# Three-pass gate products in every step, head rows scaled by another engine, and a new order of the whole run: a four-layer graph network on one core

## The chip, the cores and the metric

One Trainium2 chip, one core of it. The metric is the device time of one launch in microseconds (us). PE is the matrix engine, DVE the vector engine, ACT the scalar engine, POOL the general one, SP the engine whose queue issues nearly all transfers here. PSUM is the memory that PE writes, in eight banks[...].

## The reference, cut to what matters

Input `x` is 32 batches of 512 nodes with 128 features, and one 512x512 adjacency matrix serves all of them. Four layers follow each other, each as `x = x + layer(relu(layernorm(x)))`.

```python
# layer 0, once a batch
out = einsum('nm,bmc->bnc', A_norm, h);  out = out @ W.T + b
# layer 1, five steps a batch (in_matrix and out_matrix are both adj)
m = einsum('nm,bmd->bnd', adj, h);  av = concat([m, m]);  u3 = h @ u3_w.T + u3_b
z = sigmoid(av @ w3_w.T + w3_b + u3);  r = sigmoid(av @ w4_w.T + w4_b + u3)
hv = tanh(av @ w5_w.T + w5_b + (r * h) @ u5_w.T + u5_b)
h = (1 - z) * h + z * hv
# layers 2 and 3, attention over the edges
h = h @ W;  e = leaky_relu(e_src[:, None] + e_dst[None, :]);  softmax over the neighbours;  attn @ h
```

## The kernel before, in words

Each batch is a tile of 128x512 numbers. Layer 0 (`gcn`) and layer 1 (`ggnn`, `step`) are products with the adjacency, and layers 2 and 3 (`gat`) are attention. In all four, PE does the products, ACT what comes out of PSUM and the tanh and exp, DVE the sums and products of whole tiles and the transposes of 32x32 blocks (L592), which DMAs through DRAM finish (`shuttle`).

A product with 32-bit operands is taken at full precision (an FP32 matmul) or in three passes of reduced precision (FP32R). For three passes the moving operand is split (`operands`, L615 to L618): ACT writes `upper`, a little below the operand; DVE writes `lower`, the rest, and `across`, a mix of both. The fixed operand has been split once in the same way. PE adds the products of the uppers and of the lowers in a bank, ACT rescales the bank in place (`rescale`, L624), and PE adds the product of the across tiles. The product with the adjacency is always taken so (`in_three`, L642).

In `step`, that product, called `m`, goes into the three gate products of r, z and the candidate (`by_m`), each with a 128x128 weight. Where (batch, step) is in `SPLIT_GATES` (L29), `in_three` gives back the three split tiles instead of `m`, and the gate products are taken in three passes; elsewhere ACT copies `m` out of the bank (L653), and each gate product is a full-precision one. The products of `hT` and `rh` with their weights are at full precision in all steps (all of these run on L753). r and z share a bank: after r has been read, a split step rescales the bank back (factor 1/(1 + 1/4096)), and the product for z is added to it. Then DVE makes `rh` (L785), ACT the tanh of r, z and the candidate (L783, L790, L794), and DVE the new state (L796, L797, L799). Before the change, 84 of the 160 steps are split: steps 0, 2 and 4 of batches 2 to 29.

In `gat`, PE multiplies by the head weights (L866) into two banks of two chunks each. ACT takes the exp of three score columns (L882). In all but the last four batches, DVE then multiplies each pair of 128x128 chunks by its first exp column (L884). In the last four batches ACT does that scaling, one chunk at a time (L879). DVE makes the edge weights `e` (L907), and PE the mix (L933 and, in the last batches, L919).

The order of all instructions is fixed before the kernel runs, by the class `Plan`. Every operation has an engine, a cost and a due time, written beside it in the code. `attempt` plays the run with those costs. At each moment an engine takes the ready operation with the smallest `soon`, if buffers for it are free: eight banks, four tiles each of `upper` and `lower`, five of `across`, nine of `x`, six lanes. In the first round `soon` is the due time (or less, for operations with a long tail). In later rounds `put_off` plays the run backwards, and `soon` comes from how late each operation may be; only operations that lie after `near_end` in the plan's time (1228) take that value, and the others keep the due time. There are six rounds for each of two settings, and the order that ends first in the plan is emitted. Each engine then works through its queue in exactly that order, and waits where an operand or a buffer is not there yet. The plan's costs are 0.858 for a full-precision product of 512 columns (`MM`), 0.2325 for one pass (`MR`), 0.595 for a DVE operation on a whole tile (`V`), and 0.495 for an ACT copy (`COPY`).

The functions that the change touches, and what calls them:

Of the kernel before, what the change touches and what calls it, by code (L numbers as in the profile page):

```python
# [10 lines left out]
F32 = mybir.dt.float32  # L11
# [14 lines left out]
IDLE_FROM = 1342  # L26
RUN_UP = 8
LANES = 6
SPLIT_GATES = {(b, s) for b in range(2, 30) for s in range(STEPS) if s % 2 == 0}  # L29

# [27 lines left out]
class Plan:  # L60
# [44 lines left out]
    def run(self):  # L105


        self.before = {o: [] for o in self.ops}
        for o in reversed(self.ops):
            o.tail = o.cost + o.delay + max((q.tail for q in o.then), default=0)  # L110
            o.first, o.after = o.waits, len(o.then)
            for q in o.then:
                self.before[q].append(o)
        self.uses = {v: v.uses for o in self.ops for v in o.vals}
        best = math.inf, None
        for last, hurry in self.ends:
            for again in range(6):
                if again:
                    late = self.put_off()
                for o in self.ops:  # L120
                    if not again:

                        o.soon = min(o.due, last - o.tail * hurry)
                    else:
                        o.soon = late[o] / self.SLOT if o.at > self.near_end else o.due
                self.attempt()
                if self.end < best[0]:
                    best = self.end, [o.soon for o in self.ops]
                if self.end == math.inf:
                    break  # L130
        assert best[1], "the order has come to a stop"
        for o, soon in zip(self.ops, best[1]):
            o.soon = soon
        self.attempt()
        for o in self.order:
            o.emit()
# [134 lines left out]
def gnn_stack(ctx: ExitStack, tc: tile.TileContext, a: dict, out: bass.AP):  # L271
# [13 lines left out]
    def flat(t):  # L285
# [31 lines left out]
        "rstd": tiles(8, SMALL, "rstd"),  # L317
        "off": tiles(6, SMALL, "off"),
        "rden": tiles(3, SMALL, "rden"),
    }, [(167, 0.1), (181, 0.05)], 1228,  # L320
        IDLE_FROM, lambda v: nc.tensor.transpose(v.t[:, 0, :], ident.t, ident.t))
    op = plan.op
    MM, MM1, TURN, MR = 0.858, 0.224, 0.111, 0.2325
# [288 lines left out]
    def operands(src, given, made, due):  # L612

        upper, lower, across = Val("upper"), Val("lower"), Val("across")
        op("ACT", COPY, due - 5, lambda: nc.scalar.mul(made(upper.t), given(src.t), BELOW), r=[src], w=[upper])  # L615
        op("DVE", V, due - 5, lambda: nc.vector.tensor_sub(made(lower.t), given(src.t), made(upper.t).bitcast(F32)),  # L616
           r=[src, upper], w=[lower])
        op("DVE", V, due - 5, lambda: nc.vector.scalar_tensor_tensor(  # L618
            flat(across.t), flat(lower.t).bitcast(F32), -SPLIT, flat(upper.t).bitcast(F32), op0=ALU.mult, op1=ALU.add),
           r=[lower, upper], w=[across])  # L620
        return upper, lower, across
# [126 lines left out]
    def step(b, s, m, hT, due, lane):  # L748
        gate, r, rh, z, cand = Val("bank"), Val("r"), Val("rh"), Val("z"), Val("bank")
        split = isinstance(m, tuple)  # L750

        def weigh(p, i, moving, start=False, of=None):
            nc.tensor.matmul(flat(p.t), (of or gates).t[:, i, :], flat(moving.t), start=start, stop=True, skip_group_check=True)  # L753

        def by_m(p, i, at, start, *more):

            rest = [x for _, _, reads in more for x in reads]

            def others():
                for of, moving, _ in more:  # L760
                    weigh(p, 0, moving, of=of)
            if not split:
                def whole():
                    weigh(p, i, m, start)
                    others()
                op("PE", (1 + len(more)) * MM, at, whole, r=[m, gates, *rest], w=[p])
                return
            upper, lower, across = m
            upper_of, lower_of, across_of = of_gates

            def first_two():
                weigh(p, i - 1, upper, start, upper_of)
                weigh(p, i - 1, lower, False, lower_of)

            def third_one():
                weigh(p, i - 1, across, False, across_of)
                others()
            op("PE", 2 * MR, at, first_two, r=[upper, lower, upper_of, lower_of], w=[p])
            rescale(p, at - 5)
            op("PE", MR + len(more) * MM, at, third_one, r=[across, across_of, *rest], w=[p])  # L780

        by_m(gate, 1, due + 0.2, True, (gates, hT, [hT, gates]))
        op("ACT", A, due - 5, lambda: nc.scalar.activation(flat(r.t), flat(gate.t), AF.Tanh, bias=gate_b["w4"].t, scale=0.5),  # L783
           r=[gate, gate_b["w4"]], w=[r])
        op("DVE", V, due - 5, lambda: nc.vector.scalar_tensor_tensor(flat(rh.t), flat(r.t), 1.0, flat(hT.t), op0=ALU.add, op1=ALU.mult),  # L785
           r=[r, hT], w=[rh])
        if split:
            rescale(gate, due - 5, 1 / (1 + 1 / SPLIT))
        by_m(gate, 2, due + 0.3, False)
        op("ACT", A, due - 5, lambda: nc.scalar.activation(flat(z.t), flat(gate.t), AF.Tanh, bias=gate_b["w3"].t, scale=0.5),  # L790
           r=[gate, gate_b["w3"]], w=[z])
        hv, new = Val("hv"), Val("hT")
        by_m(cand, 3, due + 0.4, True, (u5T, rh, [rh, u5T]))
        op("ACT", A, due - 5, lambda: nc.scalar.activation(flat(hv.t), flat(cand.t), AF.Tanh, bias=gate_b["w5"].t),  # L794
           r=[cand, z, gate_b["w5"]], w=[hv])
        op("DVE", V, due - 5, lambda: nc.vector.tensor_sub(flat(hv.t), flat(hv.t), flat(hT.t)), r=[hT], w=[hv])  # L796
        op("DVE", V, due - 5, lambda: nc.vector.scalar_tensor_tensor(flat(hv.t), flat(z.t), 1.0, flat(hv.t), op0=ALU.add, op1=ALU.mult),  # L797
           r=[z], w=[hv])
        op("DVE", V, due - 5, lambda: nc.vector.scalar_tensor_tensor(flat(new.t), flat(hv.t), 0.5, flat(hT.t), op0=ALU.mult, op1=ALU.add),  # L799
           r=[hv, hT], w=[new])  # L800

        last = s == STEPS - 1
        h = Val("h", C)
        if not EARLY <= due < STEPS * B:
            p = to_features(new, due + 2, *([] if last else [h]))
            if last:
                op("DVE", V, due + 2, lambda: nc.vector.tensor_add(flat(xs[b].t), flat(xs[b].t), flat(p.t)),
                   r=[p, lane], w=[xs[b]])
            else:
                op("ACT", COPY, due + 1, lambda: nc.scalar.copy(flat(h.t), flat(p.t)), r=[p], w=[h])  # L810
            return h, False, new
        shuttle(new, "p (c q i) -> p q c i", h, due, due - 5)
        if last:
            op("DVE", V, due + 2, lambda: nc.vector.tensor_add(
                xs[b].t.rearrange("p c (k j) -> p k c j", k=Q), xs[b].t.rearrange("p c (k j) -> p k c j", k=Q),
                h.t.rearrange("p k (c j) -> p k c j", c=C)), r=[h, lane], w=[xs[b]])
        return h, True, new
# [27 lines left out]
    def gat(b, l, due):  # L845
# [14 lines left out]
        for a, q in enumerate(qs):  # L860
# [7 lines left out]
            if near:  # L868
                def scores(a=a, qt=qt, ht=ht):
                    for c in range(2):  # L870
                        nc.scalar.activation(ht()[:, c, D:D + 3], qt()[:, c, D:D + 3], AF.Exp,
                                             scale=rstd.t[:, 2 * a + c:2 * a + c + 1])
                op("ACT", 0.2, due + 1, scores, r=[q, rstd], w=[h[2 + a]])
                op("DVE", 0.08, due + 1, lambda a=a, ht=ht: nc.vector.tensor_mul(
                    g.t[:, 2 * a:2 * a + 2], ht()[:, :, D], rstd.t[:, 2 * a:2 * a + 2]), r=[rstd, h[2 + a]], w=[g[a]])

                def scale(a=a, qt=qt, ht=ht):
                    for c in range(2):
                        nc.scalar.mul(ht()[:, c, :D], qt()[:, c, :D], g.t[:, 2 * a + c:2 * a + c + 1])  # L879
                op("ACT", 2 * 0.385, due + 1.5, scale, r=[q, g[a]], w=[h[a]])  # L880
            else:
                op("ACT", 0.1, due + 1, lambda qt=qt, ht=ht: nc.scalar.activation(ht()[:, :, D:D + 3], qt()[:, :, D:D + 3], AF.Exp),  # L882
                   r=[q], w=[h[2 + a]])
                op("DVE", 0.335, due + 1.5, lambda qt=qt, ht=ht: nc.vector.tensor_mul(  # L884
                    ht()[:, :, :D], qt()[:, :, :D], ht()[:, :, D:D + 1].to_broadcast([P, 2, D])), r=[q, h[2 + a]], w=[h[a]])
        exps = [h[2], h[3]]

        row, e, mask = Val("row"), Val("e", C), (own_mask if near else maskT)[l]
# [134 lines left out]
```

## Time and profile before

| | us |
|---|---|
| median of 3 runs (1555.43 to 1557.11) | 1556.69 |
| the profiled execution, its own time | 1555.74 |
| its span, first to last instruction | 1554.0 |
| PE idle in the first 100 us | 4.96 |
| PE idle in the last 54 us | 5.4 |
| PE idle in the 1400 us between | 7.2 |

The span is the part of the time in which instructions run. An engine's busy time is the time in which at least one of its instructions is under way; instructions of one engine overlap at their ends, and a matmul's end is modelled, so a busy engine can still be held up inside it. A row of the groups gives line, engine, operation, output<-inputs, shapes, count, then busy time and mean duration of one, and the idle time of the engine just before with what ended it. A row of the timeline gives start, length, engine, line, operation, tiles and how many were merged. A row by stage gives the stretch and then, for each engine, busy us and instructions. A full-precision matmul is two records in the trace, a reduced-precision pass one. The granted PE clock is full in every slice.

### The profile page before, as it was taken

Reading aid. Unit: us, or ns where it says so; the run is one execution under the profiler, and the core shown is the slowest. Engines: PE = TensorE matmul, PEld = TensorE weight load, DVE = VectorE, ACT = ScalarE, POOL = GpSimd, SP = SyncE. Lnnn points to the kernel's source line nnn. Section 1 sums busy time; section 2 is a strip of 40 time slices with the busy share of each in tenths; the row PEclk is TensorE's granted clock in tenths of the full one; section 3 lists DMA queues with packets and bytes.
Section 4 is the critical chain, followed back from the end, with each engine's and each line's share of the span. In section 5 each row is a group of like instructions: output and inputs, shape, how many; then the busy total and the mean of one; then the engine's idle time right before and its main releaser. Section 6 shows DMA issues by size and latency. Waiting matters only on the chain.

```text
span 1554.0 us, 23910 instructions
## 1 busy us (share of the span) xinstructions
PE 1536.5 (99%) x7213; PEld 1118.2 (72%) x7213; DVE 1450.7 (93%) x3725; ACT 1048.0 (67%) x2160; POOL 155.1 (10%) x137
## 2 busy tenths in 40 slices
PE   9999999999999999999999999999999999999998
PEld 7665677777767777776777767777767776767778
DVE  8999889899999999999999999999999989978789
ACT  7867776666677576766757667676776658466574
POOL 2201000010011010111100110101010101000010
PEclk9999999999999999999999999999999999999999
DMA  3143344444354444434344444344343434523101
GB/s 109 42 99 105 78 101 114 108 117 110 95 136 108 119 114 108 124 102 122 96 111 115 122 111 114 99 120 116 102 130 90 115 92 110 131 72 105 44 13 42
DMA packets 270147, 157.72 MB, mean 101 GB/s; under 512 B 81249, under 2 KB 236225, under 8 KB 270017
## 3 DMA queue, kind: packets, MB, share of 16 engines
q1 hardware_dynamic: 269728, 155.66, 38.7%
q8 instruction: 57, 0.93, 0.3%
q10 hardware_dynamic: 288, 0.52, 0.1%
q14 instruction: 74, 0.60, 0.1%
HBM read 86.25 MB, written 69.84 MB: 100 GB/s over the span
## 4 chain that ended last, share of the span: by engine, by line
PE 62%; DVE 26%; ACT 4%; DMA 3%; issue 3%; SPq 1%; POOL 1%; DVEq 0%; POOLq 0%; ACTq 0%
PE bank L753 27%; PE bank L642 21%; PE bank L933 9%; DVE e L907 3%; DVE lower L616 3%; DVE st L507 2%; DVE across L618 2%; PE bank L866 2%; DVE sq L592 2%; DVE hv L797 1%; DVE hv L796 1%; DVE hT L799 1%; ACT bank L624 1%; POOL rstd L520 1%; DVE rh L785 1%
## 5 line engine op out<-in xcount | busy, mean ns | idle before, releaser
L624 ACT ACTIVATE bank<-bank 128x512 f32<-128x512 f32 x524 | 295.6, 582 | 174.3 <-PE bank L642 126.0
L520 POOL TENSOR_TENSOR rstd<-ve,mhalf 128x4 f32<-128x4 f32 x119 | 142.9, 1202 | 1310.9 <-DVE ve L512 954.1
L753 PE MATMUL bank<-m,wT 128*128 128x512 f32 x456 | 225.4, 595 | 4.6 <-ACT r L783 2.5
L933 PEld LDWEIGHTS bank<-h_gat,e 128*128 128x128 f32 x1792 | 210.2, 191 | 16.1 <-issue 11.0
L933 PE MATMUL bank<-h_gat,e 128*128 128x129 f32 x1792 | 212.0, 275 | 0.7 <-DVE v L938 0.4
L642 PE MATMUL bank<-adj,across 128*128 128x512 f32 x640 | 192.1, 426 | 1.1 <-ACT bank L624 1.1
L642 PE MATMUL bank<-adj,upper 128*128 128x512 f32 x640 | 192.7, 423 | 0.0
L618 DVE SCALAR_TENSOR_TENSOR across<-lower,upper 128x512 fp32r<-128x512 f32 x272 | 183.1, 678 | 3.9 <-PE bank L753 1.9
L642 PE MATMUL bank<-adj,lower 128*128 128x512 f32 x640 | 173.2, 393 | 0.0
L753 PE MATMUL bank<-rh,wT 128*128 128x512 f32 x320 | 164.0, 594 | 0.2
L753 PE MATMUL bank<-hT,wT 128*128 128x512 f32 x320 | 163.3, 592 | 0.0
L783 ACT ACTIVATE r<-bank,gate_bw 128x512 f32<-128x512 f32 x160 | 109.6, 685 | 75.4 <-PE bank L753 72.3
L907 DVE SCALAR_TENSOR_TENSOR e<-row,h_gat,maskT 128x512 f32<-128x512 f32 x224 | 157.6, 741 | 0.0
L642 PEld LDWEIGHTS bank<-adj,across 128*128 128x128 f32 x640 | 118.4, 188 | 50.3 <-issue 19.4
L642 PEld LDWEIGHTS bank<-adj,upper 128*128 128x128 f32 x640 | 118.5, 188 | 42.3 <-issue 18.9
L790 ACT ACTIVATE z<-bank,gate_bw 128x512 f32<-128x512 f32 x160 | 109.0, 685 | 51.1 <-PE bank L753 49.4
L642 PEld LDWEIGHTS bank<-adj,lower 128*128 128x128 f32 x640 | 120.0, 188 | 27.6 <-DVE lower L616 0.7
L794 ACT ACTIVATE hv<-bank,gate_bw 128x512 f32<-128x512 f32 x160 | 108.9, 685 | 41.8 <-PE bank L753 41.4
L526 ACT ACTIVATE y<-x,off,rstd 128x128 f32<-128x128 f32 x252 | 111.4, 488 | 31.9 <-DVE off L523 30.5
L796 DVE TENSOR_TENSOR hv<-hv,hT 128x512 f32<-128x512 f32 x160 | 108.6, 682 | 21.3 <-ACT hv L794 21.2
L753 PEld LDWEIGHTS bank<-m,wT 128*128 128x128 f32 x456 | 82.0, 189 | 63.8 <-issue 37.3
L753 PE MATMUL bank<-upper,gates 128*128 128x512 f32 x252 | 124.7, 495 | 0.9 <-ACT bank L624 0.9
(159 smaller groups left out, 2622.8 us busy)
## 6 DMA issues: line engine op xcount, KB each, us to landing
far<-sq SPq DMA_DIRECT2D x928, 64.0 KB
h<-far SPq DMA_DIRECT2D x148, 256.0 KB
gT<-far SPq DMA_DIRECT2D x56, 256.0 KB
row<-line SPq DMA_DIRECT2D x56, 256.0 KB
hT<-far SPq DMA_DIRECT2D x112, 64.0 KB
x<-in_x_dram SPq DMA_DIRECT2D x24, 256.0 KB
out_dram<-x SPq DMA_DIRECT2D x20, 256.0 KB
adjT<-in_x_dram SPq DMA_DIRECT2D x8, 256.0 KB
```

What stands on the lines that cost most here:

```text
L520: op("POOL", 1.0, due, lambda: nc.gpsimd.tensor_tensor(rstd.t, ve.t, mhalf.t, ALU.pow), r=[ve, mhalf], w=[rstd])
L526: op("ACT", 0.385, due, lambda c=c: nc.scalar.activation(chunk(y, c), xb.t[:, c, :], AF.Relu, bias=off.t[:, c:c + 1], scale=rstd.t[:, c:c ...
L618: op("DVE", V, due - 5, lambda: nc.vector.scalar_tensor_tensor(flat(across.t), flat(lower.t).bitcast(F32), -SPLIT, flat(upper.t).bitcast(F ...
L624: op("ACT", COPY, due, lambda: nc.scalar.mul(flat(p.t), flat(p.t), by), w=[p])
L642: nc.tensor.matmul(flat(p.t), left.t[:, c, :], right.t[:, c, :], start=first and c == 0, stop=c == C - 1, skip_group_check=True)
L753: nc.tensor.matmul(flat(p.t), (of or gates).t[:, i, :], flat(moving.t), start=start, stop=True, skip_group_check=True)
L783: op("ACT", A, due - 5, lambda: nc.scalar.activation(flat(r.t), flat(gate.t), AF.Tanh, bias=gate_b["w4"].t, scale=0.5), r=[gate, gate_b["w ...
L790: op("ACT", A, due - 5, lambda: nc.scalar.activation(flat(z.t), flat(gate.t), AF.Tanh, bias=gate_b["w3"].t, scale=0.5), r=[gate, gate_b["w ...
L794: op("ACT", A, due - 5, lambda: nc.scalar.activation(flat(hv.t), flat(cand.t), AF.Tanh, bias=gate_b["w5"].t), r=[cand, z, gate_b["w5"]], w ...
L796: op("DVE", V, due - 5, lambda: nc.vector.tensor_sub(flat(hv.t), flat(hv.t), flat(hT.t)), r=[hT], w=[hv])
L907: op("DVE", 0.65, due + 3, lambda j=j: nc.vector.scalar_tensor_tensor(e.t[:, j, :], matrix(row), h.t[:, j, D + 1:D + 2], mask.t[:, j, :], ...
L933: nc.tensor.matmul(pt()[:, c, :D + 1], e.t[:, j, i * P:(i + 1) * P], h.t[:, j, :D + 1], start=(j == 0), stop=(j == C - 1))
```

## The change

Four edits. `SPLIT_GATES` takes all five steps of batches 2 to 29, so 140 steps instead of 84 are split. The scaling of head rows in all but the last four batches goes from one DVE operation for two chunks to two ACT operations, one for each chunk. `near_end` goes from 1228 to 0, so that the backward pass gives every operation's priority, and there are eight rounds instead of six. The plan's cost of `lower` and `across` goes from 0.595 to 0.575. The function `one_pass` stands for `weigh` in the split products and issues the same matmuls.

```diff
-SPLIT_GATES = {(b, s) for b in range(2, 30) for s in range(STEPS) if s % 2 == 0}
+SPLIT_GATES = {(b, s) for b in range(2, 30) for s in range(STEPS)}
...
-            for again in range(6):
+            for again in range(8):
...
-    }, [(167, 0.1), (181, 0.05)], 1228,
+    }, [(167, 0.1), (181, 0.05)], 0,
...
-        op("DVE", V, due - 5, lambda: nc.vector.tensor_sub(made(lower.t), given(src.t), made(upper.t).bitcast(F32)),
+        op("DVE", 0.575, due - 5, lambda: nc.vector.tensor_sub(made(lower.t), given(src.t), made(upper.t).bitcast(F32)),
...
-        op("DVE", V, due - 5, lambda: nc.vector.scalar_tensor_tensor(
+        op("DVE", 0.575, due - 5, lambda: nc.vector.scalar_tensor_tensor(
             flat(across.t), flat(lower.t).bitcast(F32), -SPLIT, flat(upper.t).bitcast(F32), op0=ALU.mult, op1=ALU.add),
...
+        def one_pass(p, i, moving, start, of):
+            nc.tensor.matmul(flat(p.t), of.t[:, i - 1, :], flat(moving.t), start=start, stop=True, skip_group_check=True)
...
-                weigh(p, i - 1, upper, start, upper_of)
-                weigh(p, i - 1, lower, False, lower_of)
+                one_pass(p, i, upper, start, upper_of)
+                one_pass(p, i, lower, False, lower_of)
...
-                weigh(p, i - 1, across, False, across_of)
+                one_pass(p, i, across, False, across_of)
...
-                op("DVE", 0.335, due + 1.5, lambda qt=qt, ht=ht: nc.vector.tensor_mul(
-                    ht()[:, :, :D], qt()[:, :, :D], ht()[:, :, D:D + 1].to_broadcast([P, 2, D])), r=[q, h[2 + a]], w=[h[a]])
+                def scale(qt=qt, ht=ht):
+                    for c in range(2):
+                        nc.scalar.mul(ht()[:, c, :D], qt()[:, c, :D], ht()[:, c, D:D + 1])
+                op("ACT", 0.52, due + 1.5, scale, r=[q, h[2 + a]], w=[h[a]])
```

## The prediction, made before the changed kernel was run

> **What bounds the kernel now.** I read the page's busy times first, then the busy times by stage, the groups by line, and the timeline for the distance between starts.
>
> ```profile
> span 1554.0 us, 23910 instructions
> PE 1536.5 (99%) x7213; PEld 1118.2 (72%) x7213; DVE 1450.7 (93%) x3725; ACT 1048.0 (67%) x2160; POOL 155.1 (10%) x137
> PE 62%; DVE 26%; ACT 4%; DMA 3%; issue 3%; SPq 1%; POOL 1%; DVEq 0%; POOLq 0%; ACTq 0%
> ```
>
> PE is busy 99%, DVE 93%. The chain that ended last runs mostly through PE, and already a quarter of it through DVE. By stage, cut where the 26th and the 126th `rh` (L785) start in the timeline (252.1 and 1187.7 us, 100 gated steps or 20 batches apart), and for three single windows:
>
> ```profile
> core 0: us, PE busy (x) PEld busy (x) DVE busy (x) ACT busy (x) POOL busy (x), PEclk, DMA share, GB/s
> 0.00:252.00 252.00, 246.37 (x998) 168.30 (x998) 225.44 (x618) 184.03 (x363) 34.38 (x35) 1.00 0.36 90
> 252.00:1188.00 936.00, 931.41 (x4358) 682.22 (x4357) 899.97 (x2271) 641.87 (x1308) 90.73 (x77) 1.00 0.44 113
> 1188.00:1554.00 366.00, 358.68 (x1861) 267.66 (x1859) 325.28 (x838) 222.12 (x491) 30.03 (x25) 1.00 0.30 81
> ...
> 400.00:500.00 100.00, 99.96 (x459) 72.11 (x458) 98.03 (x251) 70.84 (x146) 11.03 (x9) 1.00 0.43 111
> 1000.00:1100.00 100.00, 100.00 (x465) 72.69 (x464) 98.04 (x257) 71.24 (x146) 10.87 (x9) 1.00 0.43 110
> ```
>
> In the middle 60% of the run DVE is busy 900 of 936 us, against 89% before and after it. DVE there has 36 us to spare, and the change takes from it. The groups concerned:
>
> ```profile
> L624 ACT ACTIVATE bank<-bank 128x512 f32<-128x512 f32 x524 | 295.6, 582 | 174.3 <-PE bank L642 126.0
> L753 PE MATMUL bank<-m,wT 128*128 128x512 f32 x456 | 225.4, 595 | 4.6 <-ACT r L783 2.5
> L618 DVE SCALAR_TENSOR_TENSOR across<-lower,upper 128x512 fp32r<-128x512 f32 x272 | 183.1, 678 | 3.9 <-PE bank L753 1.9
> L884 DVE TENSOR_TENSOR h_gat<-bank,h_gat 128x256 f32<-128x256 f32 x112 | 44.0, 409 | 0.8 <-ACT h_gat L882 0.7
> ```
>
> Rows overlap, so a mean is too long as a price; the distance between starts is the price:
>
> ```profile
> 700.07 1.88 PE L753 MATMUL bank<-m,wT 128*128 128x512 f32 x4
> ...
> 703.12 0.40 PE L753 MATMUL bank<-upper,gates 128*128 128x512 f32 x1
> ...
> 703.23 0.68 DVE L618 SCALAR_TENSOR_TENSOR across<-lower,upper 128x512 fp32r<-128x512 f32 x1
> 703.35 0.40 PE L753 MATMUL bank<-lower,gates 128*128 128x512 f32 x1
> ...
> 703.83 0.74 DVE L907 SCALAR_TENSOR_TENSOR e<-row,h_gat,maskT 128x512 f32<-128x512 f32 x1
> ```
>
> Four `m,wT` records take 1.88 us, so (1.88 - 0.595)/3 = 0.428 each; one full-precision product is two records, 0.857. A reduced-precision pass is 703.35 - 703.12 = 0.23. `across` holds DVE for 703.83 - 703.23 = 0.60, not 0.678.
>
> [...]
>
> **The change, part by part.**
>
> *Gate products on PE.* 28 batches x 2 odd steps x 3 gates = 168 products[...]: 168 x (0.857 - 3 x 0.23) = 168 x 0.167 = 28 us off PE. All on the bound engine.
>
> *What feeds them.* For each of the 56 steps: the copy of `m` (L653, 584 ns) becomes `upper<-bank` (L615, 593 ns), a wash; `lower` and `across` on DVE are new, 56 x 2 x 0.60 = +67 us; four rescales of a bank (L624; three in by_m, one that undoes it between r and z) are new on ACT, 224 x 0.49 (a pair of them lasts 1.07, one 0.58) = +110 us. Each rescale lies between two PE groups on one bank; queued behind it on ACT are tanh and relu of other lanes, for which DVE's `rh` and `hv` wait.
>
> *Head rows.* 112 DVE operations go: two `h_gat` rows together last 0.72 in the timeline, one 0.41, so about 0.32 each: -36 us on DVE. Instead ACT gets 224 scalings of 128x128 from a bank. The last four batches do that already (L879, mean 371 ns, two in a row 0.63): 0.26 each, +58 us. ACT: 1048 + 110 + 58 = 1216 us, near 79%; it stays below the other two, and costs only where its order delays someone.
>
> *DVE in sum*: +67 - 36 = +31 us, of which 20/28 or 22 in the middle stretch.
>
> *The order.* The change from 1228 to 0 lets the backward pass set the priorities of every operation, not only of late ones, and two tries are added. Instruction counts of DVE (3727), SP (1464) and POOL (142) are the same in the two built programs, so no transfer is added; all are moved. On SP the load of the w4 weights goes from third to seventh, behind two x loads and the W load; its transposes stand ahead of PE's first product (8.71 us now), so up to 1 us may be lost, or nothing if it lands in time. For the order as such I see no gain: counting passes, PE is filled 97.6% from 400 to 1200 us and about 97% from 1250 to 1500, where the backward pass worked already. Value 0, ends -6 (half of the 12 us that PE lacks work before 252 us) and +6. The costs that the planner has for `lower` and `across` fall to 0.575; the trace says 0.60, so the plan believes DVE some 600 x 0.025 = 15 us freer than it is. The pools of `upper` and `lower` stay at four for 328 uses instead of 272: 18.8 us for a use instead of 22.9. Price unknown: 0 to +8.
>
> **The sum, by stage.** I counted the instructions on each engine's queue in the two orders up to the same `rh`, and priced them with the starts above (e 0.66, transposes 0.63, bn_stats 0.19, 128-column products 0.22).
> - To the 26th `rh`: PE 239.6 before, 238.7 after. 252.1 becomes about 251.5.
> - Middle: PE 919 falls to 898, DVE 883 rises to 902 (busy 900 is longer than 883 because some 0.08 us of a row's end shows only when nothing follows it). Now PE fills 98.2% of the 935.6 us and DVE 94.3%. Afterwards DVE has more work than PE. It becomes the bound. I let it reach 97.5%, a little less than the bound engine does today, since PE must be kept at 898/925 = 97.1% at the same time; the windows from 400 and 1000 show both near that. 902/0.975 = 925 us, 11 less.
> - Rest: PE 347.5 falls to 340.1, DVE 312 rises to 321 and keeps slack: 366.3 x 340.1/347.5 = 358.5, 8 less.
>
> 251.5 + 925 + 358.5 = 1535 of span. The profiled execution took 1555.74 for a span of 1554.0, so 1.7 is outside; and it lay 0.95 below the median of 1556.69. 1535 + 1.7 + 1.0 = about 1538.
>
> **The rivals.**
> - *PE stays the bound*, DVE follows: the middle is 898/0.982 = 914, total 251.5 + 914 + 358.5 + 2.7 = 1527. For it: single 50 us stretches with DVE at 99%. Against it: 902 us of DVE in 914 is 98.7%.
> - *Looser*: DVE reaches only 96%: 902/0.96 = 940, total 1552, a third of a per cent.
> - *Slower: ACT's order starves DVE.* Each newly split step puts four more rescales on ACT's one queue, and `upper`, which opens DVE's two new operations, stands on that queue too. If DVE's filling stays at today's 94.3%, the middle is 902/0.943 = 956 and the total 1569. It decides when the filling is below 902/944 = 95.6%, at which the 8 us won at the end are eaten. For it: ACT goes from 67% to 79%, the plan underrates DVE. Against it: today DVE idles because PE is the bound, not because ACT is late (r L783 kept `rh` waiting only 13.7 us in all).
> - *The change does not do what it says*: ruled out; the built program has 420 products in three passes instead of 252, and 60 full-precision ones from `m` instead of 228.
>
> **How the numbers follow.** DVE-bound 1538: 0.43; PE-bound 1527: 0.22; looser 1552: 0.17; slower 1569: 0.18. A measurement tells 0.2% (3 us) from no change. Faster: 0.43 + 0.22 + 0.12 of the looser case = 0.77; same 0.05; slower 0.18. The range goes from the PE-bound case less the -6 of the order, 1522, to 1559, above the looser case with most of the pools' +8; it leaves out most of the slower case.
>
> **What would show it.** Right: 28 us less PE passes, DVE busy over 97% between the 26th and 126th `rh` and that stretch near 925 us, the rest near 358; waits of PE for DVE's `lower` and `across` grow. PE-bound: that stretch near 914. Slower: that stretch above 944 with DVE idle behind `upper` and ACT. I am wrong as well if the stretch before 252 us moves by more than 3 us: then the order did it.

## The result, and the profile after

The changed kernel takes 1538.89 us (median of 4 runs, 1538.19 to 1539.78) against 1556.9 before in the same comparison: a ratio of 0.9885, 95% interval 0.9868 to 0.9902. The forecast was 1538. The profiled execution took 1538.23 us, its span 1536.4. The number was met; the experiments below show that steps behind it were wrong, and what made up for them.

Busy times and the chain that ended last (the last piece of work, followed back step by step to what released it), from the page of the kernel after:

```profile
span 1536.4 us, 24733 instructions
PE 1514.7 (99%) x7373; PEld 1149.8 (75%) x7373; DVE 1475.1 (96%) x3725; ACT 1203.0 (78%) x2608; POOL 153.7 (10%) x137
...
PE 56%; DVE 29%; ACT 6%; issue 4%; DMA 3%; SPq 1%; POOL 1%; DVEq 0%; POOLq 0%; ACTq 0%
```

PE is still called 99% busy, DVE rose from 93 to 96%, ACT from 67 to 78%. The busy times by stage, cut again at the 26th and the 126th `rh` (they start at 248.5 and 1176.0 us), tell more:

```profile
0.00:248.00 248.00, 243.14 (x1017) 173.20 (x1018) 226.32 (x616) 193.88 (x384) 33.25 (x34) 1.00 0.36 89
248.00:1176.00 928.00, 917.59 (x4469) 703.63 (x4468) 915.29 (x2255) 754.54 (x1634) 90.91 (x77) 1.00 0.45 114
1176.00:1536.00 360.00, 353.94 (x1892) 272.96 (x1890) 333.54 (x858) 254.62 (x591) 29.52 (x26) 1.00 0.32 83
```

In the middle DVE (third engine of each row) is busy 915.29 of 928 us, 98.6%, where it was 900 of 936. PE was idle for 4.6 us of it before and is idle for 10.4 now. The groups that the change feeds:

```profile
L624 ACT ACTIVATE bank<-bank 128x512 f32<-128x512 f32 x748 | 426.3, 593 | 117.1 <-PE bank L642 63.3 <-PE bank L756 52.4
...
L618 DVE SCALAR_TENSOR_TENSOR across<-lower,upper 128x512 fp32r<-128x512 f32 x328 | 221.3, 681 | 2.1 <-PE bank L756 0.4
...
L756 PE MATMUL bank<-upper,gates 128*128 128x512 f32 x420 | 203.9, 486 | 4.4 <-DVE lower L616 2.0 <-ACT bank L624 1.6 <-ACT z L793 0.4
...
L889 ACT ACTIVATE h_gat<-bank,h_gat 128x128 f32<-128x128 f32 x224 | 69.8, 388 | 0.9
```

The rescales went from 524 to 748 and last 593 ns on average (582 before); the head rows are 224 ACT operations of 388 ns, where L879 had shown 371. ACT's 1203.0 us are 13 below the forecast of 1216, so these prices held.

Busy time hides how much of a run PE really lacks work: before, PE's busy time leaves 17.5 us of the span idle, the count below 43.3. So I counted it for every kernel: the matmul records of its trace times the distance between starts, as the traces of before and after have it (0.4285 us for a full-precision record of 512 columns, 0.229 for a reduced-precision pass, 0.11 for 128 to 131 columns). That is "PE work"; the span less it is what PE lost, waiting or stalled. "DVE fill" is DVE's work, counted in the same way, over the stretch from the 26th to the 126th `rh`.

| kernel | median us | PE work | PE lost | middle us | DVE fill there | chain on PE / DVE |
|---|---|---|---|---|---|---|
| before | 1556.9 | 1510.7 | 43.3 | 935.6 | 94.5% | 62% / 26% |
| after | 1538.9 | 1481.2 | 55.2 | 927.5 | 97.4% | 56% / 29% |
| e1 order alone | 1542.9 | 1509.8 | 30.6 | 936.8 | 94.8% | 77% / 15% |
| e2 all steps alone | 1563.8 | 1480.8 | 81.8 | 939.4 | 98.1% | 36% / 47% |
| e3 heads alone | 1547.2 | 1510.9 | 34.0 | 939.6 | 92.3% | 79% / 13% |
| e4 after, heads on DVE | 1553.6 | 1480.5 | 71.6 | 941.3 | 98.0% | 37% / 48% |
| e5 after, old steps | 1548.6 | 1510.7 | 35.8 | 934.3 | 92.5% | 68% / 20% |
| e6 after, old order | 1547.9 | 1480.5 | 65.2 | 939.0 | 96.6% | 34% / 43% |
| e7 after, rh doubled | 1557.6 | 1481.2 | 74.7 | - | - | 37% / 43% |
| e8 after, more PE | 1546.5 | 1498.0 | 46.9 | 932.5 | 96.9% | 68% / 21% |
| e9 after, rows after mix on ACT | 1540.4 | 1481.2 | 56.7 | 931.8 | 95.8% | 49% / 32% |
| e10 after, old costs | 1537.8 | 1481.2 | 54.8 | 927.1 | 97.1% | 39% / 40% |
| e11 before, new costs | 1563.8 | 1510.6 | 52.0 | 947.6 | 94.0% | 51% / 35% |
| e12 before, rh doubled | 1572.1 | 1510.7 | 59.3 | - | - | 35% / 47% |

(The doubled `rh` shifts the cuts, so two rows have no middle.) The cuts follow `rh`, so a new order can move work of other layers across them; then a stretch changes its length without any wait, and what PE lost in it says more. Between before and after, 29.5 us of PE work went and PE lost 11.9 us more: 17.6 us of span.

### The profile page after: what moved, and what is told of

It reads as the page before. It is cut to its first block, busy times and chain, and to the rows that moved or that the text cites. A ratio compares the mean times of both kernels' runs of the same rounds, so it can differ in the third digit from the quotient of the medians.

```text
span 1536.4 us, 24733 instructions
## 1 busy us (share of the span) xinstructions
PE 1514.7 (99%) x7373; PEld 1149.8 (75%) x7373; DVE 1475.1 (96%) x3725; ACT 1203.0 (78%) x2608; POOL 153.7 (10%) x137
## 4 chain that ended last, share of the span: by engine, by line
PE 56%; DVE 29%; ACT 6%; issue 4%; DMA 3%; SPq 1%; POOL 1%; DVEq 0%; POOLq 0%; ACTq 0%
PE bank L642 19%; PE bank L753 13%; PE bank L756 11%; PE bank L938 7%; DVE e L912 4%; DVE lower L616 4%; DVE across L618 3%; DVE sq L592 2%; DVE st L507 2%; PE bank L869 2%; ACT bank L624 2%; DVE hv L799 2%; DVE hT L802 1%; ACT y L526 1%; DVE rh L788 1%
## 5 line engine op out<-in xcount | busy, mean ns | idle before, releaser
L624 ACT ACTIVATE bank<-bank 128x512 f32<-128x512 f32 x748 | 426.3, 593 | 117.1 <-PE bank L642 63.3
L938 PEld LDWEIGHTS bank<-h_gat,e 128*128 128x128 f32 x1792 | 217.8, 191 | 21.5 <-issue 14.1
L618 DVE SCALAR_TENSOR_TENSOR across<-lower,upper 128x512 fp32r<-128x512 f32 x328 | 221.3, 681 | 2.1 <-PE bank L756 0.4
L938 PE MATMUL bank<-h_gat,e 128*128 128x129 f32 x1792 | 220.3, 275 | 0.1
L756 PE MATMUL bank<-upper,gates 128*128 128x512 f32 x420 | 203.9, 486 | 4.4 <-DVE lower L616 2.0
L756 PE MATMUL bank<-across,gates 128*128 128x512 f32 x420 | 202.3, 491 | 2.6 <-ACT bank L624 2.3
L642 PE MATMUL bank<-adj,upper 128*128 128x512 f32 x640 | 189.0, 417 | 0.6 <-ACT h_gat L889 0.4
L756 PE MATMUL bank<-lower,gates 128*128 128x512 f32 x420 | 166.4, 396 | 0.7 <-DVE lower L616 0.7
```

The lines of the kernel that those rows point to most:

```text
L618: op("DVE", 0.575, due - 5, lambda: nc.vector.scalar_tensor_tensor(flat(across.t), flat(lower.t).bitcast(F32), -SPLIT, flat(upper.t).bitca ...
L624: op("ACT", COPY, due, lambda: nc.scalar.mul(flat(p.t), flat(p.t), by), w=[p])
L642: nc.tensor.matmul(flat(p.t), left.t[:, c, :], right.t[:, c, :], start=first and c == 0, stop=c == C - 1, skip_group_check=True)
L756: nc.tensor.matmul(flat(p.t), of.t[:, i - 1, :], flat(moving.t), start=start, stop=True, skip_group_check=True)
L938: nc.tensor.matmul(pt()[:, c, :D + 1], e.t[:, j, i * P:(i + 1) * P], h.t[:, j, :D + 1], start=(j == 0), stop=(j == C - 1))
```

## The experiments

Theory A is the prediction's: PE sets the pace before; after the change DVE is full in the middle; the order by itself is worth nothing. The others are named in each expectation. Every run but e7, e8 and e12 has its order planned anew, so its time also holds the luck of one plan; e10 and e11 give two pairs that show how large that can be. The medians of before in the four comparisons lie between 1555.9 and 1556.9.

### e1: the order alone

```diff
-            for again in range(6):
+            for again in range(8):
...
-    }, [(167, 0.1), (181, 0.05)], 1228,
+    }, [(167, 0.1), (181, 0.05)], 0,
```

> The kernel before with only the new way of ordering (every operation's priority from the backward pass, eight rounds). Theory A (PE is the bound before; after the change DVE is the bound in the middle; the order is worth nothing by itself): 1557, within 6. Theory B (the new order is what makes the change faster, the rest cancels out): about 1540. Theory C (PE is the bound before and after, and part of its 28 us are lost to its waits for rescales): 1557.

Measured: 1542.87, ratio 0.9914 (0.9899 to 0.9929). Same instructions except eight fewer idle transposes, and 13 us less. Theory A's "worth nothing" falls. Theory B (about 1540) came nearest, though 13.1 us are not all of the change's 18.0; e4 decides against it. The trace shows where: PE lost 30.6 us instead of 43.3, spread over start, middle and rest (8.5, 13.6, 8.5 instead of 12.2, 17.4, 13.7). The list of waits of the kernel before, with who waited for whom, us in all, times and the longest:

```profile
PEld bank L753 <- ACT bank L624: 37.0, 84, 1.5
...
PEld bank L642 <- ACT bank L624: 10.3, 28, 1.7
...
PEld bank L753 <- DVE lower L616: 9.4, 25, 1.2
...
PEld bank L753 <- ACT m L653: 8.2, 20, 1.1
```

and the same of this run:

```profile
PEld bank L753 <- ACT bank L624: 18.0, 42, 1.3
...
PEld bank L753 <- DVE lower L616: 5.2, 12, 1.3
...
PEld bank L753 <- ACT m L653: 4.0, 11, 0.8
...
PEld bank L642 <- ACT bank L624: 2.8, 11, 0.4
```

Each of these waits of PE's weight loads for ACT has halved or better, the rescale of a bank in front of the third pass above all. These waits partly lie beside a running matmul (in the trace of before, PE is busy in 64.5 of the 74.0 us in which its weight loads wait for ACT), so they do not add up to the 13 us; they fit an order in which ACT's part is queued earlier. The two orders of ACT's queue were not compared, so this is argued.

### e2: all steps split, alone

```diff
-SPLIT_GATES = {(b, s) for b in range(2, 30) for s in range(STEPS) if s % 2 == 0}
+SPLIT_GATES = {(b, s) for b in range(2, 30) for s in range(STEPS)}
```

> The kernel before with only the split of all steps of batches 2 to 29; head rows stay on DVE, ordering as before. Theory A: DVE's work in the middle rises by 48 us to 931, at 97.5 per cent that is 955 us instead of 936, so the whole is about 1569, slower than before. Theory B: near 1557. Theory C: the same PE work as after the change, so near 1539.

Measured: 1563.83, ratio 1.0046 (1.0029 to 1.0063): slower, with 30 us less PE work. Theory A had the sign, and 5 us too much; theory C falls. Theory A put the loss in the middle (955 us), which took only 939.4 (935.6 before); more than half of the loss came in the start and the rest. By stage:

```profile
0.00:253.00 253.00, 247.47 (x1035) 175.32 (x1036) 231.45 (x634) 194.82 (x384) 33.55 (x35) 1.00 0.35 89
253.00:1193.00 940.00, 919.71 (x4448) 699.34 (x4448) 931.28 (x2323) 711.58 (x1463) 87.42 (x76) 0.99 0.44 112
```

DVE is busy 931.28 of 940 us. Its work is 921.9, a fill of 98.1%, so DVE can be filled a little more than the 97.5% of the prediction. The chain is on DVE for 47%.

### e3: head rows on ACT, alone

```diff
-                op("DVE", 0.335, due + 1.5, lambda qt=qt, ht=ht: nc.vector.tensor_mul(
-                    ht()[:, :, :D], qt()[:, :, :D], ht()[:, :, D:D + 1].to_broadcast([P, 2, D])), r=[q, h[2 + a]], w=[h[a]])
+                def scale(qt=qt, ht=ht):
+                    for c in range(2):
+                        nc.scalar.mul(ht()[:, c, :D], qt()[:, c, :D], ht()[:, c, D:D + 1])
+                op("ACT", 0.52, due + 1.5, scale, r=[q, h[2 + a]], w=[h[a]])
```

> The kernel before with only the scaling of head rows moved to ACT. Theory A: DVE is not the bound before, so 1557, at most 4 less. Theory D (relief of DVE is the whole gain, the passes saved are worth nothing): about 1539. Theory C: 1557.

Measured: 1547.15, ratio 0.9943 (0.9928 to 0.9957). Between the theories: 9 us gained by relieving an engine that was idle for 103 us of the run. PE work is the same; PE lost 34.0 us. "DVE is not the bound before" was too simple.

### e4: after the change, head rows back on DVE

The edit of e3 taken back in the kernel after.

> The kernel after the change with the scaling of head rows put back on DVE (36 us of DVE, 26 in the middle). Theory A: the middle is (902 + 26)/0.975 = 952 instead of 927, the whole about 1562. Theory C: DVE is not the bound, about 1540. Theory B: about 1540.

Measured: 1553.6, ratio to before 0.9982 (0.9976 to 0.9989), so 14.7 us longer than after the change. It is 10.7 us longer than e1, which has the same order-making and head rows, 29 us more PE work and the old costs. Theories B and C expected none of it. The move of the head rows puts some 50 us on ACT (1153.3 us busy here, 1203.0 after), and still the run is shorter with it, so ACT's amount of work is not by itself what holds up the run here. DVE's fill is 98.0%, its share of the chain 48%. Theory A has the mechanism and 8 us too much: DVE filled up to 98.0%, not 97.5%, and its work in the middle came out at 922.8, not 928.

### e5: after the change, old set of split steps

```diff
-SPLIT_GATES = {(b, s) for b in range(2, 30) for s in range(STEPS)}
+SPLIT_GATES = {(b, s) for b in range(2, 30) for s in range(STEPS) if s % 2 == 0}
```

> The kernel after the change with the old set of split steps (84, not 140): new order and head rows on ACT, and PE keeps the 28 us of passes. Theory A2 (revised after the first four runs: the new order takes some 13 us out of PE's lost time at the start and in the last fifth, and the saved passes shorten the run only until DVE is full in the middle): as the order alone or up to 3 less, 1540 to 1543, so that the saved passes are worth 1 to 4 us. Theory A as on record (order worth nothing, the passes worth 19): about 1555. Theory B: about 1540.

Measured: 1548.56, ratio 0.9949 (0.9932 to 0.9966). All expectations missed. Beside everything else the added split steps are worth 9.7 us, not 1 to 4. And this kernel, with less DVE work than e1, is 5.7 us slower than e1. It differs from e1 in the head rows and in the plan's cost of `lower` and `across`, so e10 and e11 try the costs. e3 has the same work as this run, in the old order and with the old costs, and is 1.4 us shorter: here the new order, with the new costs, brought nothing.

### e6: after the change, old way of ordering

The edit of e1 taken back in the kernel after.

> The kernel after the change with the ordering of before (backward pass only after 1228 of the plan, six rounds). Theory A2: the middle stays near 927, the start and the last fifth lose again some 10 us, so 1546 to 1552. Theory A as on record (order worth nothing): 1539, within 6. Theory E (the order's gain is only the scatter of one plan against another): anything from 1535 to 1552, and the stretches do not tell start and end from the middle.

Measured: 1547.9, ratio 0.9945 (0.993 to 0.996): the order is worth 9.0 us in the changed kernel. But the stretches are not where A2 put them: the start (246.8) is even shorter than after the change, the rest (360.0) is as long, and the middle takes 939.0 instead of 927.5. Some 5 us of that are PE work which this order has moved into the middle; counted as PE lost, the middle has 6.3 of the 10 us (36.2 instead of 29.9), the rest 2.8 and the start 1.0. PE waits for the rescales, first in this run:

```profile
PEld bank L756 <- ACT bank L624: 53.1, 112, 1.7
...
PEld bank L756 <- DVE lower L616: 15.8, 33, 1.0
...
PEld bank L642 <- ACT bank L624: 13.9, 34, 1.4
...
PEld bank L753 <- DVE rh L788: 11.3, 22, 1.6
```

and the kernel after the change:

```profile
PEld bank L756 <- ACT bank L624: 27.6, 63, 1.5
...
PEld bank L756 <- DVE lower L616: 10.2, 18, 1.7
...
PEld bank L642 <- ACT bank L624: 7.5, 17, 1.0
...
PEld bank L753 <- DVE rh L788: 7.1, 12, 1.1
```

The wait for the rescales is halved again, as between before and e1. DVE's fill under the old order is 96.6% in this run.

### e7 and e8: more DVE, more PE, in the order of after

```diff
-        op("DVE", V, due - 5, lambda: nc.vector.scalar_tensor_tensor(flat(rh.t), flat(r.t), 1.0, flat(hT.t), op0=ALU.add, op1=ALU.mult),
-           r=[r, hT], w=[rh])
+        def make_rh():
+            for _ in range(2 if s == 2 and 2 <= b < 30 else 1):
+                nc.vector.scalar_tensor_tensor(flat(rh.t), flat(r.t), 1.0, flat(hT.t), op0=ALU.add, op1=ALU.mult)
+        op("DVE", V, due - 5, make_rh, r=[r, hT], w=[rh])
```

> The kernel after the change, same order on every engine, with rh written twice in step 2 of batches 2 to 29: 28 more DVE operations, 17 us, 12 of them in the middle stretch; the result is unchanged. Theory A2 (DVE is full in the middle): 12 to 17 longer, 1551 to 1556. Theory C (PE is the bound): 0 to 4 longer.

Measured: 1557.57, 18.7 us longer for 17 us of work (28 x 0.60), 2 above A2's range.

```diff
-                for c in range(C):
+                for c in [c for _ in range(2 if 6 <= b < 25 else 1) for c in range(C)]:
                     nc.tensor.matmul(p.t[:, c, :], m.t[:, c, :], w0T.t[:, 0, :], start=True, stop=True)
```

> The kernel after the change, same order on every engine, with layer 0's product with W made twice in batches 6 to 24: 76 more full-precision products of 128 columns, 17 us of PE; the result is unchanged. Theory A2: PE goes from 897 to about 914 us of the middle's 927, that is to its own limit of 98.5 per cent, so 3 to 10 longer, 1542 to 1549. Theory C (PE is the bound): 17 longer, 1556.

Measured: 1546.52, 7.6 us longer for 17 us of PE work (1498.0 against 1481.2), within what A2 expected and far from theory C's 17. So PE alone is not the bound after the change: 17 us more of it cost less than half. The same addition to the kernel before was not run, so how far PE was the bound there is not measured in this way. PE lost 46.9 instead of 55.2 us; the chain went to PE (68%).

### e9: a further relief of DVE

```diff
+                def divide(chunks=chunks, pt=pt):
+                    for c, i in enumerate(chunks):
+                        nc.scalar.mul(v.t[:, i, :], pt()[:, c, :D], rden.t[:, i:i + 1])
...
-                op("DVE", 0.335, due + 4, lambda some=some, pt=pt: nc.vector.tensor_mul(
+                    op("ACT", 0.52, due + 4, divide, r=[p, rden[2 * a], rden[2 * a + 1]], w=[v[a]])
```

> The kernel after the change, and layer 2's division by the softmax sum in all but the last four batches (56 DVE operations of 128x256 from a bank, 0.33 each, 18.6 us, 13 of them in the middle) moved to ACT too (112 operations of 0.26, 29 us). Theory A2 (DVE is full in the middle and gives back what the saved passes are worth): DVE there falls to 890 us, at 97.4 per cent 914, where PE's own limit of 897/0.985 = 911 is near; so about 13 less than after the change, 1526, within 5 for the scatter of plans. Theory H (ACT, now near 80 per cent, is what holds PE up): 1539 or more.

Measured: 1540.38, ratio to before 0.9898 (0.9883 to 0.9913). No gain over the change; A2's 1526 is missed by 14, and theory H's "1539 or more" came true. DVE's work in the middle did fall, to 892.8, but its fill fell with it, to 95.8%. The page of this run and, from the list of groups, the new group's own wait:

```profile
PE 1514.6 (98%) x7373; PEld 1149.8 (75%) x7373; DVE 1457.4 (95%) x3669; ACT 1231.8 (80%) x2720; POOL 156.2 (10%) x137
...
L945 ACT ACTIVATE v<-bank,rden 128x128 f32<-128x128 f32 x112 | 34.6, 371 | 42.4 <-DVE rden L941 42.0
...
L968 ACT ACTIVATE r<-v 128x512 f32<-128x512 f32 x28 | 18.0, 644 | 0.3
```

ACT, 80% busy, sat idle for 42.0 us in front of these operations until DVE had made the reciprocal. In the kernel after the change ACT waited 27.3 us for DVE at this place, in front of the exp, so the move added 15 us. The head rows of the change do not have such a wait (L889: 0.9 us); what they need is made by ACT itself. But that these waits ate the gain is not shown, and the trace speaks against it: PE has no idle time inside them, its weight loads 2.8 us, and the waits of PE and its weight loads for ACT add up to 67 us here and 66 after the change. What grew is DVE's idle time, from 61 to 81 us, by as much as was taken off it; DVE's waits for ACT grew from 30 to 45. So DVE lost work and PE went no faster. DVE is then not the only bound of the changed kernel; whether ACT's part in the chains through all three engines is the other one stays open, since no run added or removed ACT work alone.

### e10 and e11: the plan's costs

```diff
-        op("DVE", 0.575, due - 5, lambda: nc.vector.tensor_sub(made(lower.t), given(src.t), made(upper.t).bitcast(F32)),
+        op("DVE", V, due - 5, lambda: nc.vector.tensor_sub(made(lower.t), given(src.t), made(upper.t).bitcast(F32)),
```

(and the same for `across`; V is 0.595)

> The kernel after the change, with the plan's cost of lower and across back at 0.595; the same instructions, another order. Theory E (plans of the same work scatter by some us, whatever way they are made): within 6 of 1539, either way. Theory G (the new cost makes a better plan): 1545 or more.

Measured: 1537.75, ratio 0.988 (0.9865 to 0.9895): 1.1 less than after the change, which their intervals do not part. Theory E holds here, theory G falls.

The opposite edit in the kernel before:

> The kernel before with only the plan's cost of lower and across at 0.575; the same instructions, another order, made in the old way. Theory E (the order of before is by accident a poor one; three other plans with its PE work lost 31 to 36 us of PE against its 43): 1543 to 1550. Theory B2 (only the backward pass over the whole run makes a better order): 1556, within 3.

Measured: 1563.78, ratio 1.0049 (1.0034 to 1.0064). The same work as before on every engine, in another order of the old making, and 7.9 us more. PE lost 52.0 us, and its chain went from 26 to 35% on DVE. The distance between starts of these operations is 0.60 in the trace of before, so the new cost is farther from the truth than the old. Theory E had expected a gain and B2 no difference; both miss. One worse plan does not show, though, that the order of before was a good one. Two orders of the same work lie 8 us apart here and 1 apart in e10; with one pair each I can't say how much is the cost and how much is scatter.

### e12: more DVE, in the order of before

The edit of e7 in the kernel before.

> The kernel before, same order on every engine, with rh written twice in step 2 of batches 2 to 29 (17 us of DVE, 12 in the middle); the result is unchanged. After the change the same addition took 18.7 us. Theory A2 (DVE is not the bound before): 0 to 6 longer, 1556 to 1562. Theory D2 (DVE already helps to set the pace before, as a quarter of its chain lies on DVE): 10 or more longer.

Measured: 1572.09, ratio 1.0104 (1.0087 to 1.0121): 16.2 us longer, nearly as after the change, though DVE was idle for 103 us of the run before and 61 after. This is what theory D2 expected. `rh` is an operation that PE's next product of the same step waits for, so both runs with it measure the length of a path through PE, ACT and DVE as much as DVE's fill; e7 alone would have been read wrongly. The traces show a part of this path: PE's weight loads waited for `rh` 6.4 us before and 16.4 in this run (7.1 after the change, 12.0 in e7).

## Why the prediction was right, and where it was not

*The work.* 28 us off PE: 29.5 by count (336 full-precision records of 0.4285 us and eight idle transposes of 0.11 fewer, 504 passes of 0.229 more). DVE's own work in the middle from 883 to 902: measured 884.5 to 903.1. ACT at 1216: 1203. These terms held.

*The middle.* Forecast 925 at a fill of 97.5%; measured 927.5 at 97.4%, with DVE busy 98.6% of it. The rival with PE as the bound, which needed 914, falls, and e8 agrees. e2 and e4 show that without the relief of DVE the three passes cost time (7.9 us alone, 10.7 in e4 against e1). The signs given for being right came: the waits of PE and its weight loads for DVE grew from 34 to 45 us and those for ACT fell from 83 to 66, though those for `lower` (11 to 14 us) grew hardly more than its uses did. With two restrictions the forecast of the middle stands. DVE's fill is not a constant to divide by: in e9 work left DVE and the fill fell. And more work on DVE costs time (the 36 us of head rows 14.7 in e4, 17 us on a waited-for path 18.7 in e7), while 18.6 us less of it gave nothing back (e9), so DVE is one of several bounds and not the only one.

*DVE before.* The prediction saw 36 us to spare on DVE in the middle and let the change take them for nothing. Relief of DVE alone gained 8.8 us (e3), and 17 us more on it cost 16.2 (e12). So DVE already helped to set the pace, and the sum by stages had no term for that.

*The rest.* Forecast 358.5, measured 360.4. The prediction counted 347.5 us of PE work there before; by the count used here it is 352.6, and it falls by 5.3 and not by 7.4.

*The start.* Forecast 251.5, measured 248.5, after 252.1. That is 3.6 us, and the prediction had named more than 3 us here as a sign that it is wrong and that the order did it. The time did not come out of waits: PE lost 12.2 us in the start before and 12.1 after, and 3.4 us less PE work lies before the cut. Under the old order (e6) the start is shorter still, 246.8, so the new order is not needed for it.

*The order at value 0, ends -6 and +6: wrong.* It is worth 13.1 us alone (e1) and 9.0 beside the rest (e6). From e2 to e4, where the costs change too, it is worth 10.2; from e3 to e5, likewise, nothing (+1.4). The argument was that PE's filling by stage looked no better after 1228, where the backward pass already had its say. (By the count used here PE is filled to 98.2% from 400 to 1200 us and 97.7% from 1250 to 1500, each some 0.6 above the prediction's figure.) That compared two stages with different work. It left out that PE's waits for ACT's rescales depend on the order: in front of the gate products they halve in e1 (37.0 to 18.0 us), and again from e6 to after (53.1 to 27.6).

*Why the number was met all the same.* This was luck in good part. I let DVE reach a fill of 97.5%, and took as support that DVE was busy 98.0% of two windows before. But busy time is longer than the work by the ends of rows (`across` before: 0.678 us a row, starts 0.60 apart), as the prediction says itself; counted like the fill, DVE's work in these windows is about 96 to 97%. Under the old order the changed kernel reaches 96.6% (e6), under the new one 97.4%. So most of the order's 9 us went into the forecast by way of an assumed fill, under another name. With the order held as it was, the same sum would have said 1538 and the chip 1547.9. The slower rival had set its point of decision at 95.6%; e6 stood 1.0 above it. The order is not all of it either: e2 reached 98.1% under the old order, with 15 us more work on DVE in the middle than e6.

*What each part is worth.* Alone, from before: order -13.1, heads -8.8, all steps +7.9, costs +7.9. Beside the other three, from after: order -9.0, heads -14.7, all steps -9.7, costs +1.1. The parts do not add up. The three passes need both others: they cost 10.7 us in the new order without the head rows (e1 to e4) and give nothing in the old order with them (+0.7, e3 to e6); with both they gain 9.7. (From e1 to e4 and from e3 to e6 the costs change too.) Most of these figures are of the size by which e11 parts two plans of the same work, so their signs hold only as far as several of them agree.

*Open.* Why the backward pass over the whole run halves the waits for ACT was not tried apart from the number of rounds. How far two orders of the same work scatter is known from two pairs only. What PE loses 55 us to after the change is not settled between DVE and ACT. Whether an order exists in which e9's relief pays was not tried; no run beat the changed kernel clearly.

## What to carry to other kernels

When an exchange takes work off the bound engine and puts it on a second one that is nearly full itself (DVE's fill was 94.5% here), sum the second engine's own work over the stretch and divide by a measured fill, not by a busy share, and give the fill a range: here it lay between 96.6 and 98.1% in the runs with all steps split and no further relief, and fell to 95.8% in e9. And try the relief of the second engine and the exchange both alone and together, since one can be a loss alone and a gain in company (here +7.9 and -9.7 us). Where the whole order is planned again, treat the order as an edit of its own with its own run: here it was worth as much as the arithmetic in three pairs of runs out of four. Before moving an operation to another engine's queue, look at who makes its operand: here one made on the same engine came without a wait (L889, 0.9 us), and one made elsewhere left ACT idle for 42 us (L945).

## What the runs showed of the hardware that I had not expected

An engine that idles for 103 us of a 1556 us run (DVE before) can still pass on 16.2 of 17 added us, here when the addition is on a path that PE waits for (e12). And the granted PE clock fell below full (0.93 to 0.97) in some windows of e2 in which PE ran short of work. Busy times of e2 in three windows of 50 us; the third number from the end is the clock:

```profile
350.00:400.00 50.00, 46.71 (x213) 34.20 (x212) 49.28 (x126) 37.24 (x79) 4.41 (x4) 0.97 0.44 110
...
900.00:950.00 50.00, 47.29 (x242) 36.11 (x241) 49.83 (x135) 35.45 (x74) 5.60 (x5) 1.00 0.39 100
...
1200.00:1250.00 50.00, 47.38 (x209) 35.77 (x208) 48.30 (x127) 36.24 (x75) 5.85 (x5) 0.93 0.30 80
```

With PE idle some 3 us in 50, the clock was 0.97 and 0.93 in two of them and full in the third, with 2.7 us idle. So idle time in this amount can come with a lower clock and need not; no rule follows from these runs. The mean of e2's profiled execution is 0.995, that of before and after 1.000. A part of e2's loss may be the clock, but hardly the most of it: in e4 the six executions at a clock of 1.000 took 1553.0 us on average and the six at 0.998 took 1554.1, which makes some 3 us for e2's 0.995 of its 7.9 (an estimate from e4's executions, which scatter by as much).
